# Local feed-forward of a four-layer model: turned tokens copied to SBUF, normalised in place behind the residual, turned back one tile later

## The chip, the cores and the metric

The kernel runs on one core of a Trainium2 chip. The metric is the device time of one execution in microseconds (us). Engines are named as in the profile: PE is TensorE, DVE is VectorE, ACT is ScalarE, POOL is GpSimd, SP is SyncE, which here only issues DMAs. PSUM is the memory that PE writes, SBUF the large on-chip memory.

## The reference

The model adds, to a float32 tensor x of 4 rows of 512 tokens with 128 features, four pairs of a conditioning layer and a feed-forward layer. The change concerns one of them, `_L2_ffn_ref`, which is itself a local transformer of depth 6 with 16 heads of 64 features and windows of 32 tokens. Cut to what matters:

```python
def ffn_layer(x, g, bln, W1, b1, W2, b2):
    mu = x.mean(-1, keepdims=True)
    var = ((x - mu) ** 2).mean(-1, keepdims=True)
    xn = (x - mu) / jnp.sqrt(var + 1e-05) * g + bln
    hg = xn @ W1 + b1
    a, gate = jnp.split(hg, 2, -1)
    return a * jax.nn.gelu(gate, approximate=False) @ W2 + b2
for i in range(DEPTH):          # 6
    x = attn_layer(shift_tokens(x), Wqkv[i], q_scale[i], k_scale[i], Wo[i]) + x
    x = ffn_layer(shift_tokens(x), ln_g[i], ln_b[i], W1[i], b1[i], W2[i], b2[i]) + x
```

`attn_layer` makes queries, keys and values, gives queries and keys unit length and a rotary turn, takes a softmax over the own and the previous window, averages the values and projects the result. `W1` has 2 x 341 columns.

## The kernel before, in words

The parts ahead of and behind the local transformer are placed by a planner with costs and due times; the change doesn't touch them. `local_transformer` is scheduled by hand: inside it, each engine executes its instructions in exactly the order in which the loop body issues them, and an instruction that waits holds up everything behind it on its engine.

The tokens of a row b are kept with features on the partitions and tokens along the free side, in `Y[b]` (128 x 513; the half that is shifted by one token lies one column further on). A tile is 128 tokens of one row at one depth, so 6 x 4 x 4 = 96 tiles. The loop over n is a pipeline of three attention stages: in one turn of the loop it works on tile n (`T`: queries and keys, rotation, lengths, values), on tile n - 1 (`T1`: transposes, scores, softmax) and on tile n - 2 (`T2`: probabilities, average, projection, residual). One turn of the loop is called a tile or a phase below.

Beside these runs the feed-forward of one row, `F`, six tiles behind, spread over four turns of the loop: `m, phase = divmod(n - 6, 4)`, so a row's period is phases 0 to 3. `ff_stage` is called twice in each turn, once early (`second` false) and once at the very end (`second` true):

- phase 0, early: `ff_moments` (four PE transposes of `Y` into PSUM, statistics on DVE: four `bn_stats` and four `bn_aggr`, then two small POOL instructions, an addition and a power, for the inverse deviation). A little later in the same turn, between `normalised(T2, 0)` and `rotate(T, 0, 1)`: `ff_norm` (four DVE instructions that read the PSUM tile and write `xn` in SBUF).
- phase 0, end: `ff_turn` (four PE transposes back, and one ACT activation that scales, shifts and writes `xnT`).
- phase 1, end: two chunks of the gate, with the gelu on ACT. Phase 2, early: the third chunk; end: two chunks of the other half, multiplied in on DVE. Phase 3, early: the third; end: the second product and the addition to `Y`.

[...]two for products (`ps_mm`, tag "mm", single banks used in turn), two for transposes and values (`ps_tr`, tag "tr"), the pair "sc" and the pair "av", each pair a single buffer. The pair "sc" serves the attention scores of `T1`, which are in it from `scores` to the end of `softmax`, and every step of the feed-forward in turn.

Lines by which the profile knows the steps: L1774 queries or keys on PE, L1776 their squares on ACT; `rotate` is L1784, L1787 and L1796 on DVE and L1797 on POOL; `normalise` is L1807 and L1808 on DVE, then twelve small POOL instructions (L1812 to L1815, three times) and four large ones (L1818); `turned` and all transposes of the attention are L582, copied by ACT in L1830 (queries, keys), L1904 (probabilities) and L1933 (attention); `values` is L1853 on PE and L1854 on ACT; scores are L1874 and L1883; softmax is L1893, L1894 on DVE and L1899 on ACT; average is L1914, `normalised` L1923 and L1924, projection L1938, residual L1945. The feed-forward: transposes L1951, statistics L510 and L512 on DVE, L514 and L515 on POOL, `ff_norm` L522, `ff_turn` L1961 and L1963, gate L1972 and L1975, the other half L1983 and L1986, second product L1995, addition L1711.

In every sixteenth turn (n % 16 == 7, also a phase 1) the next depth's weights are loaded, and in every sixteenth turn with n % 16 == 15, a phase 1, POOL makes the rotary tables of the next depth.

Of the kernel before, what the change touches and what calls it, by code (L numbers as in the profile page):

```python
# [20 lines left out]
F32 = mybir.dt.float32  # L21
# [7 lines left out]
B, S, D, SK = 4, 512, 128, 77  # L29
NT = S // 128  # L30
# [208 lines left out]
def tile_kernel(ctx: ExitStack, tc: tile.TileContext, A: dict, out: bass.AP):  # L239
    nc = tc.nc  # L240
    V, G, SC, PE, DMA = nc.vector, nc.gpsimd, nc.scalar, nc.tensor, nc.sync
# [4 lines left out]
    lnp = ctx.enter_context(tc.tile_pool(name="ln", bufs=2))  # L246
# [221 lines left out]
    def col(r):  # L468
        return cols[:, r : r + 1]
# [35 lines left out]
    def moments(src):  # L505

        st = small.tile([128, NT, 6], F32, name="ln_st")
        mv = small.tile([128, NT, 2], F32, name="ln_mv")
        for t in range(NT):
            V.bn_stats(st[:, t], src[:, t])  # L510
        for t in range(NT):
            V.bn_aggr(mv[:, t], st[:, t])  # L512
        rs = small.tile([128, NT], F32, name="ln_rs")
        G.tensor_scalar(rs, mv[:, :, 1], 1e-5, None, ALU.add)  # L514
        G.tensor_tensor(rs, rs, mhalf[:, :NT], ALU.pow)  # L515
        return mv, rs

    def layernorm(dst, src, found=None):

        mv, rs = found or moments(src)  # L520
        for t in range(NT):
            V.tensor_scalar(  # L522
                dst[:, t], src[:, t], mv[:, t, 0:1], rs[:, t : t + 1], ALU.subtract, ALU.mult
            )
# [1165 lines left out]
    def local_transformer(Y):  # L1690
        with ExitStack() as es:
# [8 lines left out]
            def pair(tag):  # L1700

                t = homes["pair"].tile([128, 2, 512], F32, tag=tag, bufs=1, name=f"ps_{tag}")
                return t
# [197 lines left out]
            def probabilities(T):  # L1901
                T.PT = tp.tile([128, LH // 2, 128], F32, name="PT", bufs=1)
                for g in range(2):
                    SC.copy(T.PT[:, 4 * g : 4 * g + 4], to_features(T.P[:, 4 * g : 4 * g + 4]))  # L1904
# [36 lines left out]
            def residual(T):  # L1941
                t = T.out
                for r, o in ((slice(0, 64), 0), (slice(64, 128), 1)):
                    dst = Y[T.b][r, 128 * T.tt + o : 128 * T.tt + o + 128]
                    V.tensor_tensor(dst, t[r], dst, ALU.add)  # L1945


            def ff_moments(F):
                F.t = pair("sc")[:, 0].rearrange("p (a b) -> p a b", b=128)
                for tt in range(NT):  # L1950
                    PE.transpose(F.t[:, tt], Y[F.b][:, 128 * tt : 128 * tt + 128], ident)  # L1951
                F.found = moments(F.t)

            def ff_norm(F):
                F.xn = lnp.tile([128, NT, D], F32, name="xn")
                layernorm(F.xn, F.t, F.found)

            def ff_turn(F):
                t = pair("sc")[:, 0]
                for tt in range(NT):  # L1960
                    PE.transpose(t[:, 128 * tt : 128 * tt + 128], F.xn[:, tt], ident)  # L1961
                F.xnT = lnp.tile([128, S], F32, name="xnT")
                SC.activation(  # L1963
                    F.xnT, t, AF.Identity, scale=col(R_LG + F.i), bias=col(R_LB + F.i)
                )
                F.h = tp.tile([128, 3, S], F32, name="fh", bufs=1)

            def ff_gate(F, *chunks):
                t = pair("sc")
                for j, c in enumerate(chunks):  # L1970
                    n, o = CH_W[c], DI + 128 * c
                    PE.matmul(t[:n, j], F.w1[:, o : o + n], F.xnT, start=True, stop=True)  # L1972
                for j, c in enumerate(chunks):
                    n = CH_W[c]
                    SC.activation(  # L1975
                        F.h[:n, c], t[:n, j], AF.Gelu, bias=col(R_B1 + (3 + c) * DEPTH + F.i)[:n]
                    )

            def ff_up(F, *chunks):
                t = pair("sc")  # L1980
                for j, c in enumerate(chunks):
                    n, o = CH_W[c], 128 * c
                    PE.matmul(t[:n, j], F.w1[:, o : o + n], F.xnT, start=True, stop=True)  # L1983
                for j, c in enumerate(chunks):
                    n = CH_W[c]
                    V.scalar_tensor_tensor(  # L1986
                        F.h[:n, c], t[:n, j], col(R_B1 + c * DEPTH + F.i)[:n], F.h[:n, c],
                        ALU.add, ALU.mult,
                    )

            def ff_down(F):
                t = pair("sc")[:, 0]
                for c in range(3):
                    n = CH_W[c]
                    PE.matmul(t, F.w2[:n, c], F.h[:n, c], start=(c == 0), stop=(c == 2))  # L1995
                add_y(F.b, t, col(R_B2 + F.i))
# [9 lines left out]

            def ff_stage(F, phase, second):
                F.w1, F.w2 = loaded[F.i][3:5]
                if phase == 0:
                    (ff_turn if second else ff_moments)(F)  # L2010
                elif phase == 1 and second:
                    ff_gate(F, 0, 1)
                elif phase == 2 and second:
                    ff_up(F, 0, 1)
                elif phase == 2:
                    ff_gate(F, 2)
                elif phase == 3:
                    ff_down(F) if second else ff_up(F, 2)
# [8 lines left out]
            for n in range(len(tiles) + 10):  # L2027
                T = tiles[n] if n < len(tiles) else None
                T1 = tiles[n - 1] if 0 <= n - 1 < len(tiles) else None
                T2 = tiles[n - 2] if 0 <= n - 2 < len(tiles) else None  # L2030
                m, phase = divmod(n - 6, 4)
                F = rows[m] if 0 <= m < len(rows) else None
                if T:
                    if n % 16 == 7 and T.i + 1 < DEPTH:
                        loaded[T.i + 1] = load(T.i + 1)
                    if n == 4:
                        fill, send, send_back = clear(lnp, 1)
                        fill(G)
                        send(DMA)
                        send_back(DMA)  # L2040
                    if n % 16 == 15 and T.i + 1 < DEPTH:
                        tabs[T.i + 1] = tables(loaded[T.i + 1][5])
                    T.before = tiles[n - 1] if T.tt else None
                    T.w, T.wv, T.wo = loaded[T.i][:3]
                    T.tabs = tabs[T.i]
                    queries_or_keys(T, 0, 0)
                if T2:
                    probabilities(T2)
                if T:
                    queries_or_keys(T, 0, 1)  # L2050
                    rotate(T, 0, 0)
                if F:
                    ff_stage(F, phase, False)
                if T2:
                    average(T2, 0)
                if T1:
                    turned(T1, 0)
                if T:
                    queries_or_keys(T, 1, 0)
                if T2:  # L2060
                    normalised(T2, 0)
                if F and phase == 0:
                    ff_norm(F)
                if T:
                    rotate(T, 0, 1)
                if T2:
                    average(T2, 1)
                if T1:
                    turned(T1, 1)
                if T:  # L2070
                    queries_or_keys(T, 1, 1)
                if T2:
                    normalised(T2, 1)
                if T:
                    rotate(T, 1, 0)
                if T2:
                    attended(T2)
                if T and T.tt == NT - 1 and n + 1 < len(tiles):
                    swap(tiles[n + 1].b)
                if T1:  # L2080
                    scores(T1)
                if T:
                    rotate(T, 1, 1)
                if T:
                    normalise(T)
                if T1:
                    softmax(T1)
                if T2:
                    project_out(T2)
                    residual(T2)  # L2090
                if T:
                    values(T, 0)
                    values(T, 1)
                if F:
                    ff_stage(F, phase, True)
# [42 lines left out]
```

## Time and profile before

| what | value |
|---|---|
| three runs | 2539.14, 2546.58, 2553.28 us (median 2546.58) |
| the profiled execution | 2546.81 us, of which span 2545.0 us |
| granted TensorE clock, mean | 0.955 |
| turns of the loop with feed-forward, from first `rotate` to first `rotate` on DVE | phase 0: 18.71 to 18.72 us in all 23 full ones; phase 1: 17.53 to 18.71; phase 2: 16.07 to 17.15; phase 3: 17.89 to 19.19 |
| busy in one period, 1264.54 to 1336.06 us (71.52 us) | PE 67.28, DVE 57.17, ACT 39.09, POOL 53.87 us |

The page gives for each engine its busy time and its share of the span. "Chain" is the work that ended last, followed back from the last instruction, at each step to what released it. In the groups and the timeline, an instruction is named by line, engine, operation, and output<-inputs with sizes in partitions x elements; "x4" are four of them in a row. Idle time stands in brackets with what ended it. Matmuls are pipelined, and the ends that the profile gives for them are modelled.

### The profile page before, as it was taken

How to read it: one execution, taken by the hardware profiler on the slowest of the kernel's cores; microseconds unless marked ns; L12 is line 12 of the kernel's file. 1: busy time of each engine (PE TensorE's matmuls, PEld its weight loads, DVE VectorE, ACT ScalarE, POOL GpSimd, SP SyncE). 2: the span in 40 equal slices, each digit the busy share in tenths (PEclk: the TensorE clock that was granted, in tenths of full speed). 3: DMA queues.
4: the chain of work that ended last, by engine and by line, in shares of the span. 5: the costliest groups of instructions: out<-in, count | busy, mean ns of one | idle time of the engine just before them, and what ended most of it. 6: DMA issues, size and time to landing. Idle time of an engine off the chain costs nothing.

```text
span 2545.0 us, 87636 instructions
## 1 busy us (share of the span) xinstructions
PE 2275.1 (89%) x37341; PEld 1472.7 (58%) x37341; DVE 1792.1 (70%) x4016; ACT 1228.5 (48%) x2161; POOL 1538.1 (60%) x2613
## 2 busy tenths in 40 slices
PE   7969799968999999999999999999999999978776
PEld 3547444536666666666666666666666666644455
DVE  5543475757787787878778787887878778737522
ACT  3622144534555555555555555555555555514322
POOL 2333303367777777777777777777777777702543
PEclk9979789989999999999999999999999999978888
DMA  6201200026211120101201121111211111011023
GB/s 165 81 27 39 67 1 2 1 58 138 72 30 34 28 77 26 34 26 34 77 25 34 28 76 34 26 32 28 77 31 29 34 28 34 26 36 49 27 67 89
DMA packets 134304, 116.20 MB, mean 46 GB/s; under 512 B 29505, under 2 KB 102700, under 8 KB 133916
## 3 DMA queue, kind: packets, MB, share of 16 engines
q1 hardware_dynamic: 128373, 102.81, 15.5%
q0 software_dynamic: 4608, 7.35, 0.9%
q8 instruction: 296, 4.85, 0.8%
q14 instruction: 92, 0.75, 0.1%
q10 hardware_dynamic: 935, 0.43, 0.1%
HBM read 42.84 MB, written 21.52 MB: 25 GB/s over the span
## 4 chain that ended last, share of the span: by engine, by line
PE 48%; DVE 31%; issue 6%; ACT 6%; POOL 6%; DMA 2%; SPq 0%; ACTq 0%; POOLq 0%; DVEq 0%
PE ps_mm L1774 6%; PE ps_tr L582 6%; DVE rc L1784 5%; DVE rs L1787 5%; DVE ss L1796 5%; PE ps_av L1938 3%; PE ps_sc L1983 3%; PE ps_tr L1853 3%; PE ps_av L1914 3%; PE ps_sc L1995 3%; DVE P L1894 2%; PE ps_sc L1883 2%; DVE la_mx L1893 2%; DVE ss L1807 2%; PE ps L1312 2%
## 5 line engine op out<-in xcount | busy, mean ns | idle before, releaser
L1797 POOL TENSOR_TENSOR rc<-rc,rs 128x512 f32<-128x512 f32 x384 | 488.2, 1273 | 281.8 <-DVE rs L1787 256.9
L1774 PE MATMUL ps_mm<-wqk,y 128*128 128x512 f32 x768 | 400.1, 604 | 35.3 <-DVE rs L1787 32.1
L1784 DVE TENSOR_TENSOR rc<-ps_mm,tabs 128x512 f32<-128x512 f32 x384 | 262.5, 684 | 204.0 <-ACT sq L1776 189.1
L1818 POOL TENSOR_TENSOR rc<-rc,rn_y 128x512 f32<-128x512 f32 x384 | 388.3, 1042 | 7.5
L1776 ACT ACTIVATE sq<-ps_mm 128x512 f32<-128x512 f32 x384 | 231.8, 604 | 177.1 <-PE ps_mm L1774 134.9
L1899 ACT ACTIVATE P<-P 128x1024 f32<-128x1024 f32 x96 | 101.5, 1057 | 435.5 <-DVE P L1894 435.5
L1787 DVE TENSOR_TENSOR rs<-ps_mm,tabs 128x512 f32<-128x512 f32 x384 | 261.6, 681 | 5.0 <-POOL rc L1797 4.7
L1796 DVE TENSOR_REDUCE ss<-sq 128x8 f32<-128x512 f32 x384 | 259.6, 676 | 0.0
L1914 PEld LDWEIGHTS ps_av<-v,PT 64*32 64x32 f32 x12288 | 140.5, 105 | 139.2 <-PE ps_tr L582 71.6
L582 PE MATMUL ps_tr<-cst,rc 128*128 128x128 f32 x1536 | 211.5, 281 | 9.8 <-POOL rc L1818 5.7
L1938 PE MATMUL ps_av<-aT,wo 128*128 128x128 f32 x1536 | 198.3, 282 | 3.5 <-issue 3.4
L1938 PEld LDWEIGHTS ps_av<-aT,wo 128*128 128x128 f32 x1536 | 179.2, 191 | 13.2 <-issue 4.6
L582 PEld LDWEIGHTS ps_tr<-cst,rc 128*128 128x128 f32 x1536 | 166.0, 141 | 29.6 <-POOL rc L1818 6.8
L1914 PE MATMUL ps_av<-v,PT 64*32 64x65 f32 x12288 | 172.6, 225 | 4.4 <-DVE attn L1924 1.1
L1774 PEld LDWEIGHTS ps_mm<-wqk,y 128*128 128x128 f32 x768 | 122.9, 193 | 80.1 <-DVE rs L1787 41.1
L1883 PE MATMUL ps_sc<-kT,qT 64*32 64x64 f32 x12288 | 145.8, 225 | 25.2 <-issue 18.4
L1017 POOL DMA_INDIRECT back<-ye,to x80 | 77.4, 968 | 141.8 <-DVE ye L1131 102.2
L1883 PEld LDWEIGHTS ps_sc<-kT,qT 64*32 64x32 f32 x12288 | 140.3, 105 | 34.9 <-issue 21.5
L1830 ACT COPY qT<-ps_tr 128x512 f32<-128x512 f32 x192 | 103.2, 589 | 91.7 <-PE ps_tr L582 89.4
L763 ACT ACTIVATE P<-ps,deltaT 77x512 f32<-77x512 f32 x192 | 115.0, 682 | 63.3 <-PE ps L757 63.2
L1830 ACT COPY kT<-ps_tr 128x512 f32<-128x512 f32 x192 | 103.2, 589 | 81.3 <-PE ps_tr L582 80.0
L1924 DVE TENSOR_TENSOR attn<-ps_av,la_den 128x512 f32<-128x512 f32 x192 | 132.8, 691 | 6.6
(391 smaller groups left out, 4449.4 us busy)
## 6 DMA issues: line engine op xcount, KB each, us to landing
v<-v SPq DMA_DIRECT2D x432, 65.0 KB
v<-v SPq DMA_DIRECT2D x96, 195.0 KB
wqk<-in_L_ffn_Wqkv_dram SPq DMA_DIRECT2D x24, 256.0 KB
sent<-xn SPq DMA_DIRECT2D x2, 2210.0 KB
xe<-sent SPq DMA_DIRECT2D x16, 260.0 KB
back<-xn SPq DMA_DIRECT2D x2, 2048.0 KB
raw<-in_L_ffn_W_dram SPq DMA_DIRECT2D x8, 512.0 KB
yb<-back SPq DMA_DIRECT2D x16, 256.0 KB
```

The lines of the kernel that those rows point to most:

```text
L582: PE.transpose(t[:, i], src[:, i], ident)
L1774: PE.matmul(t, lhs, T.w[2 * kind + c], start=True, stop=True)
L1776: SC.activation(sq, t, AF.Square)
L1784: V.tensor_tensor(a, t, bc(T.tabs[:, 2 * kind, tt], [128, 8, LD], 1), ALU.mult)
L1787: V.tensor_tensor(r.rearrange("p h (x d) -> p h x d", x=2), t.rearrange("p h (x d) -> p h x d", x=2)[:, :, ::-1], bc(T.tabs[:, 2 * kind + ...
L1796: V.tensor_reduce(T.ss[:, kind, 8 * c : 8 * c + 8], sq, AX.X, ALU.add)
L1797: G.tensor_tensor(a, a, r, ALU.add)
L1818: G.tensor_tensor(a, a, bc(y[:, o : o + 8], [128, 8, LD], 2), ALU.mult)
L1830: SC.copy(t[:, 4 * c : 4 * c + 4, lead:], to_features(T.rot[kind, c].rearrange("p (k x) d -> p k (x d)", x=2)),)
L1883: PE.matmul(T.banks[32 * w : 32 * w + 32, z, k], T.qT[r, k, 32 * w : 32 * w + 32], T.kT[r, k, 32 * w : 32 * w + 64], start=False, stop=Tru ...
L1914: PE.matmul(T.means[32 * w : 32 * w + 32, x0, k], T.PT[r, 4 * g + k, 32 * w : 32 * w + 32], (T.v1 if w % 2 else T.v2)[r, x0, 4 * g + k], s ...
L1938: PE.matmul(t, T.wo[:, c], T.aT[:, c], start=(c == 0), stop=(c == 7))
```

## The change

Three things are changed in the local feed-forward. First, `ff_moments` makes the tile `xn` in SBUF and has ACT copy the turned tokens there from PSUM; the statistics read this copy. Second, `ff_norm` normalises `xn` in place and is issued behind the residual of the same turn, instead of between `normalised(T2, 0)` and `rotate(T, 0, 1)`. Third, `ff_turn` moves from the end of phase 0 to the early call of phase 1; the end of phase 0 has no feed-forward step then. Nothing is computed that was not computed before, apart from the copy.

```diff
@@ ff_moments, ff_norm
                 for tt in range(NT):
                     PE.transpose(F.t[:, tt], Y[F.b][:, 128 * tt : 128 * tt + 128], ident)
-                F.found = moments(F.t)
+                F.xn = lnp.tile([128, NT, D], F32, name="xn")
+                SC.copy(F.xn, F.t)
+                F.found = moments(F.xn)
 
             def ff_norm(F):
-                F.xn = lnp.tile([128, NT, D], F32, name="xn")
-                layernorm(F.xn, F.t, F.found)
+                layernorm(F.xn, F.xn, F.found)
@@ ff_stage
-                if phase == 0:
-                    (ff_turn if second else ff_moments)(F)
-                elif phase == 1 and second:
-                    ff_gate(F, 0, 1)
+                if phase == 0 and not second:
+                    ff_moments(F)
+                elif phase == 1:
+                    ff_gate(F, 0, 1) if second else ff_turn(F)
@@ the loop
                 if T2:
                     normalised(T2, 0)
-                if F and phase == 0:
-                    ff_norm(F)
                 if T:
                     rotate(T, 0, 1)
...
                 if T2:
                     project_out(T2)
                     residual(T2)
+                if F and phase == 0:
+                    ff_norm(F)
                 if T:
                     values(T, 0)
                     values(T, 1)
```

## The prediction

> **What bounds the kernel now.** I read the page first, for the busy shares, the chain of waits and the costliest groups.
>
> ```profile
> PE 2275.1 (89%) x37341; PEld 1472.7 (58%) x37341; DVE 1792.1 (70%) x4016; ACT 1228.5 (48%) x2161; POOL 1538.1 (60%) x2613
> PE 48%; DVE 31%; issue 6%; ACT 6%; POOL 6%; DMA 2%; SPq 0%; ACTq 0%; POOLq 0%; DVEq 0%
> ```
>
> No engine bounds it alone: the chain changes engine, and most of it is in the local transformer's loop. So I went to the timeline, DVE first, from one first `rotate` (L1784) to the next. The feed-forward's period is four tiles long, and I call the tiles phases 0 to 3. Phase 0 takes 18.71 to 18.72 us in all 23 full rows, phase 1 17.5 (18.7 in the five that also build tables on POOL). One phase 0 and its border to phase 1, on DVE:
>
> ```profile
> 1266.34 0.88 DVE L510 BATCH_NORM_STATS2 ln_st<-ps_sc 128x6 f32<-128x128 f32 x4
> ...
> 1267.62 0.69 DVE L1924 TENSOR_TENSOR attn<-ps_av,la_den 128x512 f32<-128x512 f32 x1
> 1268.97 1.37 DVE L522 TENSOR_SCALAR xn<-ps_sc,ln_mv,ln_rs 128x128 f32<-128x128 f32 x4 [0.66 <-POOL ln_rs L515]
> 1270.25 0.68 DVE L1784 TENSOR_TENSOR rc<-ps_mm,tabs 128x512 f32<-128x512 f32 x1
> ...
> 1276.58 0.83 DVE L1807 TENSOR_SCALAR ss<-ss 128x32 f32<-128x32 f32 x1
> 1277.44 0.18 DVE L1808 TENSOR_SCALAR rn_y<-ss 128x32 int32<-128x32 int32 x1
> ...
> 1278.78 1.22 DVE L1894 TENSOR_TENSOR P<-ps_sc,la_mx 128x1024 f32<-128x1024 f32 x1
> 1279.92 0.58 DVE L1945 TENSOR_TENSOR y<-ps_av,y 64x128 f32<-64x128 f32 x2
> 1283.26 0.69 DVE L1784 TENSOR_TENSOR rc<-ps_mm,tabs 128x512 f32<-128x512 f32 x1 [2.75 <-ACT sq L1776]
> ```
>
> Columns: start, duration, instruction, and in brackets the idle time before it and what ended it. See that DVE never rests within the phase but for 0.66 us, waiting for POOL's power (L515) before `ff_norm`; and that it then idles 2.75 us at the border, until ScalarE's square. What ScalarE does there:
>
> ```profile
> 1280.04 1.06 ACT L1899 ACTIVATE P<-P 128x1024 f32<-128x1024 f32 x1 [5.67 <-DVE P L1894]
> 1281.00 1.05 ACT L1854 COPY v<-ps_tr 128x512 f32<-128x512 f32 x2
> 1281.95 0.79 ACT L1963 ACTIVATE xnT<-ps_sc,cols 128x512 f32<-128x512 f32 x1
> 1282.62 0.60 ACT L1776 ACTIVATE sq<-ps_mm 128x512 f32<-128x512 f32 x1
> ```
>
> The border is a chain: DVE's subtraction ends (call this moment P, 1280.00), then exp, two copies of values, `xnT`, square, and only then the next `rotate`. PE waits for DVE twice in this phase, so it is not the bound there:
>
> ```profile
> 1271.59 1.12 PE L1774 MATMUL ps_mm<-wqk,y 128*128 128x512 f32 x2 [1.00 <-DVE rs L1787]
> ...
> 1280.15 0.63 PE L1961 MATMUL ps_sc<-cst,xn 128*128 128x128 f32 x4 [1.09 <-DVE P L1894]
> ```
>
> And POOL around P, for what follows:
>
> ```profile
> 1276.09 1.27 POOL L1797 TENSOR_TENSOR rc<-rc,rs 128x512 f32<-128x512 f32 x1 [0.51 <-DVE rs L1787]
> ...
> 1281.45 0.25 POOL L1815 TENSOR_TENSOR rn_y<-rn_y,rn_t 128x32 f32<-128x32 f32 x1
> 1281.78 4.04 POOL L1818 TENSOR_TENSOR rc<-rc,rn_y 128x512 f32<-128x512 f32 x4
> ```
>
> [...]the same operation takes 404 ns from PSUM (L522) and 342 from SBUF (L550), where four back to back took 1.11 us against 1.37. [...]L1807 takes 828 ns on average where its neighbour L1808 takes 182, and in the phase shown it ends at 1277.39, just after POOL's L1797 (1276.09 + 1.27 = 1277.36). But the trace also has L550 running at 340 ns beside POOL's power, so not every POOL instruction blocks. The changed `ff_norm` becomes just this kind of operation.
>
> **The change, part by part, for one row (24 rows, 23 of them with full phases).**
> 1. `ff_norm` leaves its place in DVE's queue: 1270.25 − 1268.97 = 1.28 us of work and 0.66 of waiting. Together −1.94. DVE was the late one there (PE's 1.00 wait behind it), so all that follows moves up: POOL's additions follow DVE's rotations by their own waits, and PE's scores end 2 us ahead of the maximum that reads them (1275.36 against 1277.51).
> 2. The new ScalarE copy: transposes end at 1265.98, ScalarE's square began at 1265.64 and the next instruction can follow 0.48 later, 1266.12; a 128x512 copy takes 0.59 (row L1830), so it ends at 1266.71. DVE was ready for the statistics at 1266.34. Their wait moves from PE to ScalarE and grows: +0.40 with the hand-over. Behind it stand `normalised` and `rotate`, all of DVE. ScalarE itself idled 1.16 us there before its qT copy, so nothing is late behind the copy. Statistics from SBUF cost the same (278 against 283 ns). The power's 1.04 us now runs beside `normalised` and `rotate`; POOL next had 2.74 us idle.
> 3. `xnT` leaves the border: 1282.62 − 1281.95 = 0.67 us. −0.67, if the next square then starts at P + 1.95 and `rotate` at P + 2.59 instead of 3.26. PE's values products end by then: they lay 0.9 us ahead of P. PE no longer waits 1.09 for the bank and runs the next queries early; next late is exp, then the copies of values.
> 4. `ff_norm` goes behind the residual, from P + 0.50. Free DVE time there up to P + 2.59 is 2.09 us; four SBUF operations take 1.11 undisturbed. Cost nothing, cover 0.98. Without it (against POOL, see rivals) each us beyond P + 2.59 delays DVE by one. It waits for POOL's power, long done. No DMA is added or moved, and SP's queue is untouched.
> 5. The transposes (0.47 on PE) and `xnT` go into phase 1's first slot, before `average`. In PE's queue behind them stand both averages, for which DVE's `normalised` waits. PE in phase 1 follows from P: probabilities from P + 1.1, queries, then the turn, first average to P + 4.3, q's transposes, queries, second average to about P + 7.05; DVE wants it at P + 2.59 + 4.42 = 7.01. Bounds: 0 if PE keeps its hidden gaps, 0.45 if POOL's L1818 is late too. I take +0.15 for the 18 ordinary phases. ScalarE had 0.69 idle there against 0.67 of new work: nothing.
> 6. In the five phases 1 with tables, DVE stands waiting for POOL (0.97 us, `rs` before POOL's addition), which starts from P's chain and isn't earlier: part 3 is lost there, 5 × 0.67 = 3.4 us.
> 7. The last row runs alone after the tiles, each step serial: +0.6 for the copy, once.
>
> Sum: 23 × (1.94 − 0.40 + 0.67) = 50.8 saved; less 18 × 0.15 = 2.7, 3.4 and 0.6, leaves 44.1. For small collisions between `ff_norm` and POOL's 0.25 us instructions I take off 0.1 a row, 2.3: about 42. The profiled execution took 2546.81 us (span 2545.0); the median of the runs is 2546.58, the same, so no scaling: 2505.
>
> **Rivals.**
> - *`ff_norm` caught behind POOL's multiplications (the other side).* L1818 starts at P + 1.78 and is four tensor-tensor instructions of 1.04, of the kind behind which L1807 waited. If k of the four DVE operations each wait for one of them, `ff_norm` ends at P + 1.78 + 1.3 k (1.04 and 0.26 of its own), later than P + 2.59 by 1.3 k − 0.81. Against about 1.85 saved a row: k = 1 costs 0.5, leaving 2546.8 − 42 + 11 = 2516; k = 2 costs 1.8, 2545, no change; k = 3 costs 3.1, 2505 + 71 = 2576, slower. It turns at two operations caught. For it: L1807. Against: `ff_norm` begins 1.28 us before L1818, needs 1.11[...].
> - *The border gains nothing, PE takes over.* PE shows 16.99 us busy of phase 1's 17.54. If the turn's 0.5 us there goes fully into the path, part 3 is lost (23 × 0.67 less the 3.4 counted already = 12) and part 5 comes to 0.45 (18 × 0.3 = 5 more): 2522. For it: that share. Against: the page warns that matmul ends are modelled, and the phase's matmul starts, added at their own spacing, make about 15.7 us.
> - *The copy only moves the wait.* If DVE's new wait for ScalarE were as long as the 0.66 it replaces plus more (1.2 us, one qT copy in front), 23 × 0.8 = 18 less: 2523. The built order has the copy ahead of the qT copies, which speaks against it.
> - *The change does not do what it says*: the built order shows `ff_norm` behind the residual and the turn in the next tile, so I give this nothing.
>
> **How the numbers follow.** Forecast (2494 to 2512): 0.58. One operation caught behind POOL, PE taking over, or the copy's wait, 2512 to 2530: 0.26. Two caught, within 0.5% (12.7 us, about what a measurement of this kernel tells from no change): 0.07. Three or more caught: 0.09. The low end takes all of the 50.8 at no cost, 2496, and a little for the clock; the high end covers the middle group. Range 2494 to 2528 leaves about 0.17 outside. Faster 0.84, same 0.07, slower 0.09.
>
> **What would show it.** Phase 0 from first `rotate` to first `rotate` at about 16.5 us instead of 18.71; no wait on POOL's L515 any more, a wait of about 0.4 on ScalarE before the statistics; the idle time before phase 1's `rotate` at about 1 us (2.75 − 0.67 − 1.11), still ended by the square; phase 1 at 17.5 to 17.7. Wrong, if L522 now takes much over 1.2 us for four, ending with POOL's L1818, if L1818 starts later than P + 2, or if phase 1 grows by more than 0.3.

## The result and the profile after

Four runs each: 2506.36 us median (2504.74 to 2508.41) against 2547.47 (2539.14 to 2553.28), a ratio of 0.9839 with a 95% interval of 0.9816 to 0.9862. The profiled execution took 2504.74 us, its span is 2503.0. The first lines of the page, busy times and the chain:

```profile
PE 2254.2 (90%) x37341; PEld 1471.1 (59%) x37341; DVE 1791.1 (72%) x4016; ACT 1243.5 (50%) x2185; POOL 1542.9 (62%) x2613
PE 57%; DVE 20%; issue 8%; POOL 7%; ACT 5%; DMA 3%; SPq 1%; ACTq 0%; POOLq 0%; DVEq 0%
```

The busy times hardly moved: DVE does the same work, ACT 15 us more (24 copies). What moved is the chain: DVE's share fell from 31% to 20%, PE's rose from 48% to 57%. The local loop, summed by phase from the DVE timeline (first `rotate` to first `rotate`):

| part | before | after | difference |
|---|---|---|---|
| phase 0, 23 rows (median 18.71, then 16.43) | 430.4 | 379.0 | −51.4 |
| phase 1, 22 rows (17.54, then 18.19; with tables 18.71, then 19.48) | 392.4 | 406.6 | +14.2 |
| phases 2 and 3 | 759.2 | 759.0 | −0.2 |
| up to the loop and its first six turns | 625.4 | 622.4 | −3.0 |
| from the last first `rotate` to the end of the span | 337.5 | 335.9 | −1.7 |

The change works where it was expected to, and phase 1 gives more than a quarter of it back. Phases 2 and 3, which the change doesn't touch, stayed as they were, so a difference in speed between the two executions does not explain the gain. DVE in one phase 0 after and at the start of its phase 1 (start, duration, instruction, idle time before and what ended it):

```profile
1182.13 0.87 DVE L510 BATCH_NORM_STATS2 ln_st<-xn 128x6 f32<-128x128 f32 x4 [0.33 <-ACT xn L1953]
...
1192.55 1.22 DVE L1894 TENSOR_TENSOR P<-ps_sc,la_mx 128x1024 f32<-128x1024 f32 x1
...
1194.29 1.12 DVE L522 TENSOR_SCALAR xn<-xn,ln_mv,ln_rs 128x128 f32<-128x128 f32 x4
1196.35 0.69 DVE L1784 TENSOR_TENSOR rc<-ps_mm,tabs 128x512 f32<-128x512 f32 x1 [0.95 <-ACT sq L1776]
...
1198.66 0.21 DVE L1923 RECIPROCAL la_den<-ps_av 128x8 f32<-128x8 f32 x1 [0.42 <-PE ps_av L1914]
```

The wait for POOL's power is gone; a wait of 0.33 us for the copy has come. `ff_norm` lies in the border's idle time and leaves 0.95 us of the 2.75. P is 1193.77 here (1192.55 + 1.22), so the next `rotate` comes at P + 2.58. The new wait is the last line: 0.42 us for PE's first average. PE at the same place:

```profile
1193.01 1.02 PE L1774 MATMUL ps_mm<-wqk,y 128*128 128x512 f32 x2
1195.39 1.14 PE L582 MATMUL ps_tr<-cst,P 128*128 128x128 f32 x8 [1.35 <-ACT v L1854]
1196.37 1.02 PE L1774 MATMUL ps_mm<-wqk,y 128*128 128x512 f32 x2
1197.23 0.60 PE L1962 MATMUL ps_sc<-cst,xn 128*128 128x128 f32 x4
1197.76 0.86 PE L1914 MATMUL ps_av<-v,PT 64*32 64x65 f32 x64
```

PE finishes its queries early, as foreseen, but then stands 1.35 us, not for exp but for a copy of the values (L1854). The moved transposes (L1962) follow, and only then the average. The two places before the change, PE and then DVE (P is 1280.00 there):

```profile
1281.62 1.14 PE L582 MATMUL ps_tr<-cst,P 128*128 128x128 f32 x8
...
1285.05 0.20 DVE L1923 RECIPROCAL la_den<-ps_av 128x8 f32<-128x8 f32 x1
```

The transposes of the probabilities began at P + 1.62 both times. DVE's L1923 began 1.79 us after the first `rotate` (1283.26), without a wait; after the change it begins 2.31 us after it.

### The profile page after: what moved, and what is told of

Read it like the earlier page. It is cut to its first block, busy times and chain, and to the rows that moved or that the text cites. A ratio compares the mean times of both kernels' runs of the same rounds, so it can differ in the third digit from the quotient of the medians.

```text
span 2503.0 us, 87683 instructions
## 1 busy us (share of the span) xinstructions
PE 2254.2 (90%) x37341; PEld 1471.1 (59%) x37341; DVE 1791.1 (72%) x4016; ACT 1243.5 (50%) x2185; POOL 1542.9 (62%) x2613
## 3 DMA queue, kind: packets, MB, share of 16 engines
q8 instruction: 296, 4.85, 0.8%
## 4 chain that ended last, share of the span: by engine, by line
PE 57%; DVE 20%; issue 8%; POOL 7%; ACT 5%; DMA 3%; SPq 1%; ACTq 0%; POOLq 0%; DVEq 0%
PE ps_tr L582 9%; PE ps_mm L1774 8%; PE ps_av L1938 4%; PE ps_tr L1853 4%; PE ps_av L1914 4%; PE ps_sc L1883 3%; DVE rc L1784 3%; DVE rs L1787 3%; DVE ss L1796 3%; PE ps_sc L1984 3%; PE ps_sc L1996 3%; PE ps L1312 2%; DVE P L1894 2%; PE ps L773 2%; DVE la_mx L1893 2%
## 5 line engine op out<-in xcount | busy, mean ns | idle before, releaser
L1797 POOL TENSOR_TENSOR rc<-rc,rs 128x512 f32<-128x512 f32 x384 | 488.6, 1276 | 230.6 <-DVE rs L1787 186.5
L1818 POOL TENSOR_TENSOR rc<-rc,rn_y 128x512 f32<-128x512 f32 x384 | 388.8, 1044 | 7.5
L1784 DVE TENSOR_TENSOR rc<-ps_mm,tabs 128x512 f32<-128x512 f32 x384 | 262.4, 683 | 160.9 <-ACT sq L1776 145.6
L1776 ACT ACTIVATE sq<-ps_mm 128x512 f32<-128x512 f32 x384 | 231.0, 602 | 152.3 <-PE ps_mm L1774 104.4
L1787 DVE TENSOR_TENSOR rs<-ps_mm,tabs 128x512 f32<-128x512 f32 x384 | 261.5, 681 | 5.9 <-POOL rc L1797 5.8
```

Source lines behind the costliest of these rows:

```text
L1776: SC.activation(sq, t, AF.Square)
L1784: V.tensor_tensor(a, t, bc(T.tabs[:, 2 * kind, tt], [128, 8, LD], 1), ALU.mult)
L1787: V.tensor_tensor(r.rearrange("p h (x d) -> p h x d", x=2), t.rearrange("p h (x d) -> p h x d", x=2)[:, :, ::-1], bc(T.tabs[:, 2 * kind + ...
L1797: G.tensor_tensor(a, a, r, ALU.add)
L1818: G.tensor_tensor(a, a, bc(y[:, o : o + 8], [128, 8, LD], 2), ALU.mult)
```

## The experiments

The edits below are against the changed kernel unless said otherwise. e1 to e4 ran on a chip where the kernel before took 2606.74 us, e5 to e8 on one where it took 2552.88, and e9, e10 and the changed kernel again on one where it took 2553.89. On the first the parts outside the loop are longer (the loop starts at 557 us in e1, 526 in the changed kernel), while the phases 0 agree within 0.02 us wherever a kernel leaves them alone. So the evidence is the phases, as medians (phase 1 without the five that make tables), and the ratio to the kernel before on the same chip.

| kernel | phase 0 | phase 1 | ratio to before |
|---|---|---|---|
| before | 18.71 | 17.54 | 1 |
| changed | 16.43 | 18.19 | 0.9839 [0.9816, 0.9862] |
| e1 turn late | 16.42 | 17.77 | 0.9817 [0.9790, 0.9845] |
| e2 turn back | 17.45 | 17.73 | 0.9858 [0.9825, 0.9890] |
| e3 norm back | 18.19 | 18.20 | 0.9996 [0.9978, 1.0014] |
| e4 statistics from PSUM | 16.44 | 18.20 | 0.9833 [0.9802, 0.9865] |
| e5 turn late, statistics first | 16.02 | 17.77 | one run |
| e6 norm in phase 1 | 16.42 | 20.51 | one run |
| e7 turn late, spare bank | 16.43 | 18.65 | one run |
| e8 e5 and e7 | 16.03 | 18.65 | 0.9881 [0.9858, 0.9903] |
| e9 the kernel of e5, five runs | 16.02 | 17.75 | 0.9776 [0.9758, 0.9794] |
| e10 e8 mended | 16.02 | 17.55 | 0.9776 [0.9762, 0.9790] |
| changed, again | 16.43 | 18.20 | 0.9835 [0.9816, 0.9854] |

**e3: does DVE bound phase 0?** `ff_norm` goes back.

```diff
                 if T2:
                     normalised(T2, 0)
+                if F and phase == 0:
+                    ff_norm(F)
...
                     residual(T2)
-                if F and phase == 0:
-                    ff_norm(F)
```

> Only ff_norm goes back to its place between normalised and the second rotation of phase 0; it still works in place in SBUF, and the turn stays in phase 1. Theory A (DVE bounds phase 0): 1.11 us of work and 0.6 to 0.7 us of waiting for POOL's power return to DVE's queue, phase 0 grows from 16.43 to about 18.2, time about 2506 + 23 x 1.75 = 2546 (2538 to 2550), nearly the time of before. Theory B (PE bounds phase 0 once xnT is gone from the border): phase 0 grows by 0.6 at most, time 2506 to 2520.

Phase 0 grew by 1.76 us and the gain was gone (0.9996). DVE in e3:

```profile
1226.62 1.11 DVE L522 TENSOR_SCALAR xn<-xn,ln_mv,ln_rs 128x128 f32<-128x128 f32 x4 [0.65 <-POOL ln_rs L515]
1227.65 0.68 DVE L1784 TENSOR_TENSOR rc<-ps_mm,tabs 128x512 f32<-128x512 f32 x1
```

Of the 1.76, the four SBUF operations are 1.03 (1226.62 to 1227.65); the rest comes with the wait for the power. DVE bounds phase 0; theory B falls. In this kernel phase 1 keeps its 18.20, although `ff_norm` is no longer at the border: the loss in phase 1 is not a collision of `ff_norm` with POOL.

**e2: is the border ScalarE's chain?** The turn goes back to the end of phase 0.

```diff
-                if phase == 0 and not second:
-                    ff_moments(F)
-                elif phase == 1:
-                    ff_gate(F, 0, 1) if second else ff_turn(F)
+                if phase == 0:
+                    (ff_turn if second else ff_moments)(F)
+                elif phase == 1 and second:
+                    ff_gate(F, 0, 1)
```

> Only the turn goes back to the end of phase 0; ff_norm stays behind the residual and the copy stays. Theory A (the border is a chain of ScalarE: exp, values, xnT, square): xnT can now start only after ff_norm and the transposes, at about P + 2.25, so the next rotate comes at about P + 3.5 instead of P + 2.6: phase 0 grows from 16.43 to about 17.4, phase 1 falls back to 17.55, net +0.35 us a row, time about 2514 (2509 to 2520). Theory B (the turn at the border is covered by other work and only its place in phase 1 costs): phase 0 stays at 16.4 to 16.6 and the time falls to about 2492.

Phase 0 came to 17.45, as theory A said. ACT at that border in e2:

```profile
1237.24 1.06 ACT L1899 ACTIVATE P<-P 128x1024 f32<-128x1024 f32 x1 [5.16 <-DVE P L1894]
1238.20 1.05 ACT L1854 COPY v<-ps_tr 128x512 f32<-128x512 f32 x2
1239.26 0.78 ACT L1964 ACTIVATE xnT<-ps_sc,cols 128x512 f32<-128x512 f32 x1
1240.17 0.60 ACT L1776 ACTIVATE sq<-ps_mm 128x512 f32<-128x512 f32 x1
```

`xnT` stands again between the values and the square, and the square starts 2.93 us after exp's start; in the changed kernel it was 1.91 (1193.80 to 1195.71). Phase 1 fell to 17.73, not to 17.55: in e2 the turn's transposes wait for `ff_norm`, and those of the probabilities behind them start only at P + 2.71. That this is the reason was not tested.

**e1: what does the turn cost in phase 1?** It goes behind the averages.

```diff
-                elif phase == 1:
-                    ff_gate(F, 0, 1) if second else ff_turn(F)
+                elif phase == 1 and second:
+                    ff_gate(F, 0, 1)
...
+                if F and phase == 1:
+                    ff_turn(F)
                 if T2:
                     attended(T2)
```

> The turn (four PE transposes and the xnT activation) goes from ahead of the first average of phase 1 to just ahead of the attention's transposes in the same phase; all else as in the changed kernel. Theory A: phase 1's growth of 0.65 us (18.19 against 17.54) is the turn's 0.5 us of PE time standing ahead of both averages, which DVE waits for. Then phase 1 falls to about 17.55, DVE's 0.4 us wait for the average before L1923 is gone, and the time is 2506 - 22 x 0.6 = about 2493 (2489 to 2497). Theory B: the growth comes from POOL, whose chain ff_norm holds up at the border, or from xnT in ScalarE's queue: then phase 1 stays at 18.1 to 18.2 and the time at 2503 to 2509.

Phase 1 fell by 0.42 us to 17.77: theory A for two thirds of the 0.65. DVE's wait before L1923 is gone; it begins 1.87 us after the first `rotate`. The whole time does not tell the two kernels apart (0.9817 against 0.9839, with intervals that overlap), so the phase is the evidence. About 0.2 stayed, so another cause had to be found. PE's line above suggested one: the transposes of the probabilities wait (1.35 us) for a `ps_tr` bank that the values occupy.

**e7 and e8: a first try at that, a miss.** In phase 1 the probabilities go to the pair "sc", which is free there in e1. The diff shows what comes on top of e1.

```diff
+                both = pair("sc").rearrange("p g (i q) -> p g i q", q=128) if spare else None
                 for g in range(2):
...
+                        t = both[:, g]
+                        for i in range(4):
+                            PE.transpose(t[:, i], src[:, i], ident)
...
+                    SC.copy(T.PT[:, 4 * g : 4 * g + 4], t)
```

> As e1, but in phase 1 the transposed probabilities go to the pair sc, which is free there, instead of the two ps_tr banks that the values have just filled. Theory A: the rest of phase 1's growth (17.77 against 17.54) is PE, whose probabilities' transposes wait for ScalarE's copies of the values to free a ps_tr bank, at P + 1.6, and not for exp, which ends at P + 1.1; then they start 0.5 us earlier and phase 1 falls to about 17.55. Theory B: the rest is ScalarE's queue (probabilities' copies behind values and square) or POOL: phase 1 stays at 17.7 to 17.8.

> e5 and e7 together: turn late, statistics from PSUM ahead of the copy, probabilities of phase 1 in the spare pair. If the three gains add up: phase 0 about 16.1, ordinary phases 1 about 17.55, so against the changed kernel 23 x 0.33 + 17 x 0.64 = 18 us less, ratio to before about 0.977 (0.974 to 0.980). If phase 1 is held by ScalarE: ratio about 0.979 to 0.981.

Phase 1 grew to 18.65 in both. PE in e7 shows why:

```profile
1211.64 0.66 PE L1909 MATMUL ps_sc<-cst,P 128*128 128x128 f32 x4 [0.88 <-ACT P L1899]
1213.58 0.66 PE L1909 MATMUL ps_sc<-cst,P 128*128 128x128 f32 x4 [1.28 <-ACT PT L1912]
```

The first four do start when exp lets them. The second four wait 1.28 us, for the copy of the first four: the pair is one buffer, and the loop issued copy and transposes in turn. So the miss was in the edit, and left the theory open.

**e10: the same, mended.** All eight transposes are issued ahead of the first copy; otherwise as e8.

```diff
+                if spare:
+                    both = pair("sc").rearrange("p g (i q) -> p g i q", q=128)
+                    for k in range(8):
+                        PE.transpose(both[:, k // 4, k % 4], T.P[:, k], ident)
```

> As e8, with all eight transposes of the probabilities of phase 1 issued ahead of the first copy, so that the second four no longer wait for it (the wait that lengthened phase 1 in e7 and e8). Theory A (PE's late start at the ps_tr bank is the rest of phase 1's growth): the transposes run at P + 1.1 to P + 2.1, ordinary phases 1 fall from 17.77 to about 17.55, phase 0 stays at 16.02, and the time lies 17 x 0.2 = 4 us below e9, ratio to before about 0.975. Theory B (ScalarE's order holds the first average): phase 1 stays at 17.7 to 17.8 and the time at that of e9.

PE in e10:

```profile
1198.13 1.09 PE L1906 MATMUL ps_sc<-cst,P 128*128 128x128 f32 x8 [0.74 <-ACT P L1899]
```

Now they wait for exp alone (they start at P + 1.14), and phase 1 is 17.55, the 17.54 of before. That settles the other part of the loss in phase 1: the bank. The time did not follow: 2496.94 us against 2494.41 for e9, with the same ratio. Summed over e10's profile, phase 1 is 1.5 us shorter than in e9, but phases 2 and 3 together are 2.3 us longer (12 of the 22 phases 2 take more than 16.2 us, 8 in e9), and the part ahead of them 4.7 us. Why was not tried.

**e4, e5 and e9: the wait for the copy.** In e4 the statistics read PSUM, in e5 they are also issued first (with the turn as in e1); e9 is e5 again. The diff is that of e5; e4 changes only what `moments` reads.

```diff
-                SC.copy(F.xn, F.t)
-                F.found = moments(F.xn)
+                F.found = moments(F.t)
+                SC.copy(F.xn, F.t)
```

> Only the statistics read PSUM again, beside ScalarE's copy, which then serves ff_norm alone. Theory A: the wait of 0.33 us for the copy before the statistics goes, phase 0 falls from 16.43 to about 16.1, time about 2506 - 23 x 0.33 = 2498 (2495 to 2502). Theory B: reads of the same PSUM bank by ScalarE and DVE are kept apart, as the rotation's first multiplication waits for the square of the same bank: DVE still waits for the copy, phase 0 stays at 16.4 and the time at 2504 to 2509.

> As e1 (turn late), and the statistics read PSUM and are issued ahead of ScalarE's copy. Theory A: e4 kept the wait because of two readers of one PSUM bank the one issued second waits for the first (there DVE for ScalarE); with the statistics first DVE waits for PE alone and starts 0.33 to 0.4 us earlier: phase 0 about 16.05 to 16.1 instead of 16.43, phase 1 as e1 at about 17.77. Theory B: the wait is one for PE's transposes in any case, phase 0 stays at 16.4.

> The kernel of e5 again, timed in rounds: turn late, statistics from PSUM ahead of the copy. From the phases of e5 (phase 0 16.02, phase 1 17.77 ordinary) against the changed kernel: 23 x 0.41 + 17 x 0.42 = 17 us less, ratio to before about 0.977 (0.974 to 0.980), if phases 2 and 3 and the rest don't give it back; if they do, 0.982 to 0.985 as the changed kernel.

> The changed kernel itself, in the same rounds, as the measure for the other two: ratio to before about 0.984 by the first comparison, phases 0 and 1 at 16.43 and 18.19.

DVE in e4, then ACT in e9:

```profile
1214.15 0.89 DVE L510 BATCH_NORM_STATS2 ln_st<-ps_sc 128x6 f32<-128x128 f32 x4 [0.33 <-ACT xn L1953]
```

```profile
1182.91 0.58 ACT L1954 COPY xn<-ps_sc 128x512 f32<-128x512 f32 x1 [1.01 <-DVE ln_st L510]
1183.39 1.08 ACT L1830 COPY qT<-ps_tr 128x512 f32<-128x512 f32 x2
```

In e4 DVE waits for ACT's copy although it reads nothing that the copy writes (0.33 us); phase 0 stays at 16.44, theory B. With the order turned, ACT waits 1.01 us for DVE's statistics, and that costs DVE nothing: phase 0 falls to 16.02. So in e4 and e9, of the two engines that read this PSUM tile, the one issued second waited for the first; whether the hardware needs this was not tried. The wait that ends the border's idle time has the same form: `rotate` (L1784) reads only `ps_mm`, yet it starts when the square (L1776), which reads that tile too, has ended (1196.35 in the changed kernel, where the square runs from 1195.71 to 1196.32). To issue `rotate` first was not tried either. e9, with both edits, took 2494.41 us where the changed kernel took 2511.04 on the same chip, and the intervals of their ratios don't overlap: it beats both kernels.

**e6: what would a collision with POOL cost?** As e1, with `ff_norm` behind the first rotation of phase 1, beside POOL's four multiplications.

```diff
-                if F and phase == 0:
-                    ff_norm(F)
                 if T:
                     values(T, 0)
...
+                if F and phase == 1:
+                    ff_norm(F)
                 if T2:
                     average(T2, 0)
                 if T1:
```

> As e1, but ff_norm goes behind the first rotation of phase 1, at about P + 4.4, while POOL runs its four L1818 multiplications (P + 1.85 to P + 5.9) and then its additions. [...] Theory A (each DVE operation waits for the POOL instruction in progress): ff_norm takes 2.5 us or more in place of 1.11, and phase 1 comes to 19.5 or more instead of 17.77. Theory B (they hardly disturb each other): ff_norm takes 1.1 to 1.3 us and phase 1 comes to about 18.6 to 18.9.

Phase 1 grew from 17.77 to 20.51. DVE, then POOL, in one of them:

```profile
1223.10 3.05 DVE L522 TENSOR_SCALAR xn<-xn,ln_mv,ln_rs 128x128 f32<-128x128 f32 x4
```

```profile
1220.50 4.04 POOL L1818 TENSOR_TENSOR rc<-rc,rn_y 128x512 f32<-128x512 f32 x4
1224.48 0.13 POOL L1847 MEMSET v<- 128x16 f32 x1
1224.55 1.26 POOL L1797 TENSOR_TENSOR rc<-rc,rs 128x512 f32<-128x512 f32 x1
```

The same four instructions took 3.05 us in place of 1.11, with starts at 1.80, 2.24, 3.24 and 4.51 us into the phase. Taken singly they lasted 0.52, 1.14, 1.35 and 0.34 us: the first three end 0.08 us behind a POOL instruction (the third L1818, the MEMSET behind the fourth, and L1797), and the fourth runs while POOL is idle. POOL itself lost nothing (4.04). Theory A holds in its sizes, for three of the four. One run gave 2561.18 us where the kernel before took 2552.88 on that chip: with `ff_norm` moved a little further, the change seems to lose all it brings, and the 2.74 us a phase agree with that.

## Why the prediction was right, and where its sum was not

The time, 2505 against 2506.36, is nearer than its terms deserve: the mechanism in phase 0 and at the border was right, one term was not, and luck made up for it. Point by point:

- *Parts 1, 2 and 3* held. Per row, the stretch from `normalised` to the second rotation shrank from 2.63 to 0.61 us (−2.02 for −1.94), the statistics start 0.41 later (for +0.40), and P to `rotate` went from 3.25 to 2.58 (−0.67 for −0.67). Sum over 23 rows 51.4, predicted 50.8. e3 and e2 show the first and the third by undoing them alone; e2's 1.02 is more than 0.67 because there the turn also waits for `ff_norm`. Two readings, the end of L1807 (1277.40) and the start of the maximum (1277.53), are off by 0.01 and 0.02 us, which changes nothing.
- *Part 4* held: `ff_norm` took 1.11 to 1.12 us at the border and delayed nothing, with 0.95 us of cover left where 0.98 was worked out. The 0.1 us a row set aside for collisions, an allowance of the author's that no trace of before had shown, was not needed in phase 0; POOL's multiplications began at P + 1.85 instead of P + 1.77. Its rival rested on L1807, which in both kernels ends 0.03 to 0.05 us behind POOL's L1797, in all 96 turns; that this would hold for `ff_norm` beside L1818 was the author's estimate. The rival was real in kind: in e6 the three operations caught took 0.44, 1.00 and 1.27 us from start to next start, for the 1.3 assumed for each.
- *Part 5* is the term that was mis-sized: +0.15 us a row, bounded by 0.45, and 0.65 measured, more than the 0.3 that the prediction itself named as a sign of being wrong. The step that failed is "probabilities from P + 1.1", with its first average to P + 4.3. In the trace those transposes start at P + 1.62 and the average ends at P + 4.85 (1197.76 + 0.86 − 1193.77), about 0.5 later than DVE wants it (P + 2.58 + 1.79). Part 3 names the copies of values as late, but part 5 followed only the data, exp's result, and left out the bank: both `ps_tr` banks hold values until ACT has copied them, and PE stood 1.35 us for that copy. Before, the start at P + 1.62 did not show as a wait, because PE had waited 1.09 us for the pair "sc" and then had queries to do up to 1281.64 (P + 1.64). Without the first wait it stood idle up to the same moment (the 1.35 us), and there was no room for the turn. Taken away one after the other, the turn's place is worth 0.42 (e1) and the bank about 0.2 (e10). The turn early with the bank free was not run, so how much each costs alone stays open.
- *Part 6*: phase 1 with tables grew by 0.77 for 0.67, as POOL sets its pace: DVE's wait there before L1787 is still for POOL (1.05 us for 0.97), and POOL's multiplications begin 0.08 later. With the turn moved away (e1) and the bank freed (e10) it stays at 19.5.
- *Part 7* can't be seen: the stretch behind the last first `rotate` is 1.7 us shorter.
- The sum came out because phase 1 cost 14.2 instead of 8.4 with the collision allowance (2.7 + 3.4 + 2.3), while the parts ahead of these turns and behind them ran 4.7 us shorter, which no step claimed and nothing here explains. In the profile of the changed kernel run again, the same parts are shorter by another 2.6 us (958.3, then 955.7), so they move by themselves. This is luck.
- Of the rivals, "PE takes over" was partly true: the border's gain of 0.67 a row is real in phase 0, and PE gives 0.65 back one phase later. What the kernel keeps is about the size of DVE's part.

## What to carry to other kernels

When a chain is shortened, ask which buffer the next engine needs and who frees it, not only which data: PE was free early here, and that was worth nothing while both transposing banks held values (it stood 1.35 us). Look at the queue of the place to which work is moved; here half a microsecond of transposes was free behind two averages (phase 1 at 17.55 in e10, 17.54 before) and cost 0.42 ahead of them (e1). Where a trace shows two engines that read one tile waiting for each other, issue first the one that is short of time: from e4 to e5, that took 0.42 us from phase 0 (16.44, then 16.02).

## What had not been expected of the hardware

First, the sizes in e6. Beside POOL's instructions on 128x512, three DVE operations with one tensor source, from SBUF to SBUF, took 0.52, 1.14 and 1.35 us, where one takes 0.34 in the changed kernel (median of its 96). POOL's four instructions kept their 4.04 us, so the waiting in e6 was all on DVE's side.

Second, not every POOL instruction did this. At the border of the changed kernel the same four operations run among POOL's instructions on 128x32 in 1.12 us. The first began at 1194.29, while an L1812 of POOL ran from 1194.20 to 1194.44, and took its usual 0.35 us. Only one POOL instruction there grew, an L1814 of 0.35 us in place of 0.29. What makes the difference was not tried.
